# A GRU's x products as seven block products for four steps, with the head's weight transfers and the order of z's sigmoid changed

## The chip, the cores and the metric

The kernel runs on one core of a Trainium2 chip. The metric is the device time of one execution in microseconds (us); the median of three runs is compared. A profiled execution gives the span (first to last instruction of the program) and what every engine did in it: PE is the matrix engine (PEld its weight loads), DVE the vector engine, ACT the scalar engine, POOL the GpSimd engine, SP the engine whose queue issues most transfers.

## The reference

A GRU runs over the 256 time steps of x for 16 sequences with 512 features. Its states go through a router and one expert matrix: each of the 16 experts takes the 256 tokens (of 4096) with the largest router weight, and what they make of them is added to x. The program's own sizes are B = 16, T = 256, D = 512.

```python
def cell(h, x):
    gi = x @ W_ih + b_ih
    gh = h @ W_hh + b_hh
    i_r, i_z, i_n = jnp.split(gi, 3, axis=-1)
    h_r, h_z, h_n = jnp.split(gh, 3, axis=-1)
    r = jax.nn.sigmoid(i_r + h_r)
    z = jax.nn.sigmoid(i_z + h_z)
    n = jnp.tanh(i_n + r * h_n)
    h_new = (1.0 - z) * n + z * h
...
S = jax.nn.softmax(xf @ router_w + router_b, axis=-1)
G, idx = jax.lax.top_k(S.T, k)
out = jnp.einsum('ekh,hd->ekd', xf[idx], expert_w) + expert_b
y = y.at[idx.reshape(-1)].add((G[..., None] * out).reshape(-1, h))
return x + y
```

All of it is float32. The expert's matrix is the same for all experts, so a token's product with it is made once and multiplied by the sum of its gates.

## The kernel before

**Tiling.** Features lie on partitions. The contraction of 512 is four parts k of 128. The matrix engine is used as four column quadrants j of 32: each matmul has 32 stationary columns (or 16 in even steps of the h product), two time steps of 16 sequences, and four of them stand side by side, so that the output's 512 columns fold into 4 x 128. Each float32 matmul is two instructions in the trace. A gate's sums of one pair of steps are a 128 x 128 block of a PSUM bank; the three h banks (r, n, z) hold two such blocks, for even and odd pairs p.

**Head** (L238 to L269, and the block that begins at L443). The weights W_ih (`wih`, four parts k, each in two half transfers by `load_k`) and W_hh (`whh`, three gates, each in two half transfers by `load_gate`) are issued on the queues of SP and ACT, with x's groups 0 and 1 (a group g is eight steps), the state and the biases. PE turns group 0 (`spread_x`), multiplies it by the parts of W_ih as they come (L403), forms the biases, turns group 1 and makes pair 4's product. Pair 5's product is spread over the first four steps of the loop. `make_masks` stands behind the head.

**Loop** (256 steps s; pair p, odd or even; group g, place c in it). The order of PE, ACT, DVE, POOL and SP is the order of the program's text. In a step:

- PE: `h_part` (L426), 96 instructions of 128 columns: gates r and n for the first two k, r and n for the other two, then z for all four. Then half of an x product for the pair six ahead, `x_part` (L403), 16 instructions of 384 columns into `x_bank0` or `x_bank1`. Then units of expert work (`expert`, L370): a unit is one k and a quarter of the columns, 8 instructions of 128. The variable `due` sets how many are made. The next step's h matmuls are queued behind them.
- ACT: r's sigmoid (L505), the copy of the next pair's preset into the r bank (`preset_first`, L386), two halves of tanh (L557), z's sigmoid in one piece (L558), the presets of n and z (`preset_rest`, L389 and L396), `gather` (L293), which copies finished states into `ht`.
- DVE: a one-element copy `seen` (L509) that waits for r, r times h's n in halves (L553), plus x's n (L555), the transposes of n (`turn_n`, L565) and z (`turn_z`, L568), h - n (`less_n`, L571), times z (`by_z`, L576), plus n (`plus_n`, L579), which writes the new state `hs`. Every one of these goes by halves of the features; a step's first h matmuls need half 0, the later ones half 1. Then, every other step, `x_done` (L414), which adds the bias to x's sums and puts them into `ring`, six pairs deep; the transposes of later groups of x (`turn_x`, L228); `expert_done`, which empties expert sums.

Of the 32 groups of tokens, the first 15 (`early_groups`) have their expert product made in the loop; the other 17 (`late_items`) after it by `late_part` (L108): some in quarters of 128 columns beside the search for each expert's smallest chosen weight (`by_bits`), the others, once the gates are known, in 512 columns at a time, from whose sums `store` (L713) writes the output.

Of the kernel before, what the change touches and what calls it, by code (L numbers as in the profile page):

```python
# [17 lines left out]
def kernel(  # L18
# [37 lines left out]
    GH = P // E  # L56
    ident = const.tile([P, P], F32, name="ident")
# [8 lines left out]
    def make_masks():  # L66
# [3 lines left out]
        at = xs[:, RING - 3, 0:3].bitcast(I32)  # L70
# [3 lines left out]
        at_f = xs[:, RING - 2, 0:3]  # L74
        nc.vector.tensor_copy(at_f, at)
        to_i = xs[:, RING - 2, P : 3 * P].bitcast(I32).rearrange("p (o e h) -> p o e h", o=2, h=GH)
        nc.gpsimd.iota(to_i[:, 0, :, :], pattern=[[1, E], [0, GH]], base=0, channel_multiplier=0)
        nc.gpsimd.iota(to_i[:, 1, :, :], pattern=[[0, E], [1, GH]], base=0, channel_multiplier=0)
        to = xs[:, RING - 3, P : 3 * P].rearrange("p (o n) -> p o n", o=2)
# [12 lines left out]
    early_groups = list(range(15))  # L92
# [65 lines left out]
    with (  # L158
# [17 lines left out]
        )  # L176
        rb = wts.tile([P, E], F32, name="rb")

        b_raw = xs[0:2, RING - 8 : RING - 5, :]
        b_n = xs[0:1, RING - 5, :]  # L180
        c0 = xs[0:B, RING - 4, :]
# [15 lines left out]

        def load_rows(dst, src, form):

            rows = src.rearrange(form, c=KC)  # L200
            for h in range(2):
                ks = slice(KC // 2 * h, KC // 2 * (h + 1))
                queues[h].dma_start(out=dst[:, ks, :], in_=rows[:, ks, :])
# [32 lines left out]
        xa2 = xs[:, RING - 9, :].rearrange("p (q d) -> p q d", d=P)  # L236
        with tc.manual_schedule(engines={ET.SP, ET.Activation, ET.Pool}):
            def load_gate(dst, src, form, i, gate):  # L238
                load_rows(dst[:, :, i, :], src[:, gate * D : (gate + 1) * D], form)

            def load_k(k):
                rows = w_ih.rearrange("(p c) n -> p c n", c=KC)
                to = wih.rearrange("p c g d -> p c (g d)")
                for h, queue in enumerate(queues):
                    cols = slice(3 * HD * h, 3 * HD * (h + 1))
                    queue.dma_start(out=to[:, k, cols], in_=rows[:, k, cols])

            nc.sync.dma_start(out=xs[:, 0, :], in_=x[:, 0:TG, :])
            load_k(0)
            nc.scalar.dma_start(out=c0, in_=cond)  # L250
            load_k(1)
            load_k(2)
            nc.scalar.dma_start(out=xs[:, 1, :], in_=x[:, TG : 2 * TG, :])
            load_k(3)
            for gate in (0, 2, 1):
                load_gate(whh, w_hh, "(c p) n -> p c n", gate, gate)
# [7 lines left out]
            for j in range(KC):  # L264
                load_xa(2, xa2, j, (nc.sync, nc.sync))
# [621 lines left out]
```

## Time and profile before

| | us |
|---|---|
| median of 3 runs | 1167.44 (1166.04 to 1168.17) |
| the profiled execution | 1166.15 |
| its span | 1164.4 |
| PE busy, matmuls | 1148.1 (99%) |
| PE busy, weight loads | 925.2 (79%) |
| DVE busy | 769.0 (66%) |
| ACT busy | 387.0 (33%) |
| POOL busy | 42.5 (4%) |
| first h matmul of the loop starts | 26.13 |
| r's sigmoid of the last step starts | 1089.87 |
| the copy of the gates (L707) starts | 1126.35 |

A group line of the page names the source line, engine and operation, output and inputs, shapes and count; then busy time, the mean of one in ns, the engine's idle time ahead of these instructions and what ended most of it. A line of the timeline has the start, the time from the first start to the last end of a merged run of instructions, and the same names; in brackets the idle time ahead of it and its releaser. Matmuls overlap each other: a duration is that of one from start to end, not the distance to the next.

### The profile page before, as it was taken

The numbers are of one execution on the slowest core, as the hardware profiler recorded it, in microseconds if no ns is written. First come the engines' busy times: TensorE is split into PE (matmuls) and PEld (weight loads), VectorE is DVE, ScalarE is ACT, GpSimd is POOL, SyncE is SP. The second block draws the span as 40 slices with busy tenths as digits, with TensorE's granted clock in tenths as the row PEclk, the third lists the DMA queues.
The fourth block names the chain that finished last, engine by engine and source line by source line (L and its number), as shares of the span: only waits on it lengthen the run. The fifth ranks groups of instructions, "written<-read, shape, count | busy, mean of one in ns | idle before, by whom it ended". The sixth has DMA issues, their size and how long they took to land.

```text
span 1164.4 us, 72051 instructions
## 1 busy us (share of the span) xinstructions
PE 1148.1 (99%) x32271; PEld 925.2 (79%) x32271; DVE 769.0 (66%) x4229; ACT 387.0 (33%) x1590; POOL 42.5 (4%) x240
## 2 busy tenths in 40 slices
PE   8999999999999999999999999999999999998898
PEld 4778888888888888888888888888888888888762
DVE  2666667666666666666676666666666666665674
ACT  1233333333333333333333333333333333333420
POOL 1000000000000000000000000000000000000000
PEclk9999999999999999999999999999999999999999
DMA  8100000000000000000000000000000000000126
GB/s 268 38 13 17 21 20 19 16 21 22 20 20 21 19 20 17 21 22 20 20 19 20 19 18 20 22 21 20 20 20 19 20 8 13 4 5 4 48 69 227
DMA packets 43818, 37.02 MB, mean 32 GB/s; under 512 B 6992, under 2 KB 35424, under 8 KB 43504
## 3 DMA queue, kind: packets, MB, share of 16 engines
q1 hardware_dynamic: 41808, 28.89, 8.4%
q8 instruction: 255, 4.18, 1.5%
q10 hardware_dynamic: 1568, 3.44, 0.9%
q14 instruction: 59, 0.48, 0.1%
q0 software_dynamic: 128, 0.02, 0.1%
HBM read 23.94 MB, written 8.39 MB: 28 GB/s over the span
## 4 chain that ended last, share of the span: by engine, by line
PE 95%; DVE 3%; DMA 1%; ACT 1%; issue 0%; SPq 0%; ACTq 0%; DVEq 0%
PE gates L426 57%; PE gates L403 27%; PE pe L108 5%; PE pe L370 5%; DMA wih<-in_L_cond_W_ih_dram 1%; PE gates L305 1%; DVE zT L568 0%; DVE nT L565 0%; DVE t L553 0%; ACT r L505 0%; ACT t L557 0%; DVE hs L579 0%; DVE v L576 0%; PE idle L403 0%; DVE u L571 0%
## 5 line engine op out<-in xcount | busy, mean ns | idle before, releaser
L426 PE MATMUL gates<-whh,hs 128*16 128x128 f32 x24576 | 724.7, 273 | 5.0 <-DVE zT L568 2.5
L426 PEld LDWEIGHTS gates<-whh,hs 128*16 128x16 f32 x24576 | 672.0, 103 | 37.6 <-ACT ht L293 15.8
L403 PE MATMUL gates<-wih,xt 128*32 128x384 f32 x4064 | 379.6, 486 | 1.9 <-DMA wih<-in_L_cond_W_ih_dram 1.6
L505 ACT ACTIVATE r<-gates 128x128 f32<-128x128 f32 x256 | 71.1, 278 | 551.9 <-PE gates L426 551.7
L403 PEld LDWEIGHTS gates<-wih,xt 128*32 128x32 f32 x4064 | 144.4, 110 | 91.4 <-issue 84.3
L509 DVE COPY seen<-r 1x1 f32<-1x1 f32 x256 | 36.3, 142 | 268.0 <-ACT r L505 267.9
L557 ACT ACTIVATE t<-t 128x64 f32<-128x64 f32 x512 | 103.2, 249 | 136.1 <-DVE t L555 136.1
L565 DVE STREAM_TRANSPOSE nT<-t 128x64 f32<-128x64 f32 x512 | 100.4, 234 | 47.8 <-ACT t L557 47.8
L568 DVE STREAM_TRANSPOSE zT<-zs 128x64 f32<-128x64 f32 x512 | 122.7, 240 | 0.6 <-ACT zs L558 0.6
L370 PEld LDWEIGHTS pe<-ewr,ht 128*32 128x32 f32 x1920 | 69.1, 110 | 62.3 <-issue 60.1
L579 DVE TENSOR_TENSOR hs<-v,nT 128x32 f32<-128x32 f32 x512 | 98.3, 192 | 17.4
L576 DVE TENSOR_TENSOR v<-u,zT 128x32 f32<-128x32 f32 x512 | 98.7, 193 | 8.8
L370 PE MATMUL pe<-ewr,ht 128*32 128x128 f32 x1920 | 92.0, 273 | 0.7 <-issue 0.7
L555 DVE TENSOR_TENSOR t<-t,xs 128x64 f32<-128x64 f32 x512 | 90.7, 219 | 0.0
L553 DVE TENSOR_TENSOR t<-r,gates 128x64 f32<-128x64 f32 x512 | 90.3, 218 | 0.0
L571 DVE TENSOR_TENSOR u<-hs,nT 128x32 f32<-128x32 f32 x512 | 78.2, 153 | 0.0
L558 ACT ACTIVATE zs<-gates 128x128 f32<-128x128 f32 x256 | 71.2, 278 | 1.8 <-ACT t L557 0.6
L414 DVE TENSOR_TENSOR xs<-gates,bias 128x384 f32<-128x384 f32 x127 | 69.7, 551 | 0.5 <-PE gates L403 0.5
L108 PE MATMUL pe<-ewr,ht 128*32 128x128 f32 (+2 forms) x1320 | 64.3, 343 | 0.0
L108 PEld LDWEIGHTS pe<-ewr,ht 128*32 128x32 f32 x1320 | 36.9, 110 | 20.5 <-issue 18.5
L293 ACT COPY ht<-hs 128x128 f32<-128x128 f32 (+1 forms) x128 | 52.2, 410 | 0.8 <-DVE hs L579 0.8
L228 DVE STREAM_TRANSPOSE xt<-xa 128x256 f32<-128x256 f32 x58 | 38.7, 668 | 6.5 <-issue 6.5
(106 smaller groups left out, 300.0 us busy)
## 6 DMA issues: line engine op xcount, KB each, us to landing
out_dram<-xs SPq DMA_DIRECT2D x31, 256.0 KB, 3.7
xa<-in_x_dram SPq DMA_DIRECT2D x232, 32.0 KB, 1.9
xs<-in_x_dram SPq DMA_DIRECT2D x100, 64.0 KB, 2.2
xs<-in_x_dram SPq DMA_DIRECT2D x6, 256.0 KB, 3.9
wih<-in_L_cond_W_ih_dram ACTq DMA_DIRECT2D x4, 384.0 KB, 7.9
wih<-in_L_cond_W_ih_dram SPq DMA_DIRECT2D x4, 384.0 KB, 10.7
whh<-in_L_cond_W_hh_dram SPq DMA_DIRECT2D x3, 512.0 KB, 12.8
whh<-in_L_cond_W_hh_dram ACTq DMA_DIRECT2D x3, 512.0 KB, 9.6
```

Of the source, the lines that this page charges most:

```text
L108: nc.tensor.matmul(pe[q, cols], ht[:, g, k, q], ewr[:, k, E:][:, cols], start=False, stop=(k == KC - 1), tile_position=(0, QD * j), skip_g ...
L370: nc.tensor.matmul(pes[g][quadrant(j), at : at + P], ht[:, g, k, quadrant(j)], ewr[:, k, E + P * quarter : E + P * (quarter + 1)], start=F ...
L403: nc.tensor.matmul(bank[quadrant(j), at], lhs, columns(wih[:, k, gates, :].rearrange("p g d -> p (g d)"), j), start=start and k == 0, stop ...
L426: nc.tensor.matmul(dst[quadrant(j, m)], lhs, columns(whh[:, k, gate_, :], j), start=False, stop=(k == KC - 1), tile_position=(0, QD * j), ...
L553: nc.vector.tensor_tensor(t[half], r[:, cols], hn[p % 2][:, cols], ALU.mult)
L555: nc.vector.tensor_tensor(t[half], t[half], ring[:, p % AHEAD, 2, cols], ALU.add)
L557: nc.scalar.activation(t[half], t[half], AF.Tanh)
L565: nc.vector.transpose(nT[half], t[half])
L568: nc.vector.transpose(zT[half], zs[:, halves[half][1]])
L571: nc.vector.tensor_tensor(u[half], hs[:, halves[half][2], slot(s), :], of_step(nT[half], odd), ALU.subtract)
L576: nc.vector.tensor_tensor(v[half], u[half], of_step(zT[half], odd), ALU.mult)
L579: nc.vector.tensor_tensor(hs[:, halves[half][2], slot(s + 1), :], v[half], of_step(nT[half], odd), ALU.add)
```

## The change

- **x products.** For four steps (two pairs, a `quad`), x's 2 x 2 blocks (pairs by halves of the features) times W_ih's 2 x 2 blocks (halves of the features by halves of the columns) are made from seven products of blocks and not eight, in Winograd's form of Strassen's scheme. A product has two k and 192 columns in four quadrants. Sums and differences of weight blocks (`t1`, `t2`, `nt4`, and one in place) are made once in the head on POOL (`mixes`); those of x's blocks for a group of eight steps on DVE (`x_sums`). The partial sums live in five PSUM regions (`a_sum`, `b_sum`, `c_sum`, `d_sum`, `e_sum`), which ACT copies from one to the next and into `ring`; `x_rest` adds the last ones on DVE. `x_done` and the pair-wise `x_part` remain in the head only, for pairs 0 to 3.
- **Expert work.** `early_groups` becomes the first 10 groups. A unit is one k and 384 or 128 columns. `due` grows by 3 in each third step of four, and by 3 or 6 in the last eight steps.
- **z.** Its sigmoid goes by halves, each behind that half's tanh, and the order of DVE's transposes, differences and products is another.
- **Head.** W_ih in four whole transfers, W_hh in three, x's group 1 behind them on SP's queue, the state on POOL's; pair 4's and pair 5's products and the early load of group 2 are gone; `make_masks` stands first.
- **Other moves.** x's transposes, loads, gathers, router products and the emptying of expert sums take place in other steps.

```diff
-    early_groups = list(range(15))
+    early_groups = list(range(N_EARLY))
...
+            nc.gpsimd.dma_start(out=c0, in_=cond)
             nc.sync.dma_start(out=xs[:, 0, :], in_=x[:, 0:TG, :])
-            load_k(0)
-            nc.scalar.dma_start(out=c0, in_=cond)
-            load_k(1)
-            load_k(2)
-            nc.scalar.dma_start(out=xs[:, 1, :], in_=x[:, TG : 2 * TG, :])
-            load_k(3)
-            for gate in (0, 2, 1):
-                load_gate(whh, w_hh, "(c p) n -> p c n", gate, gate)
+            load_k(0, nc.scalar)
+            load_k(1, nc.sync)
+            load_k(2, nc.scalar)
+            load_k(3, nc.sync)
+            load_gate(0, nc.scalar)
+            load_gate(2, nc.sync)
+            load_gate(1, nc.scalar)
+            nc.sync.dma_start(out=xs[:, 1, :], in_=x[:, TG : 2 * TG, :])
...
+        def mixes(part):
+
+            b11, b12 = (wih[:, 0:2].rearrange("p k g d -> p k (g d)")[:, :, cols] for cols in (low, high))
+            b21, b22 = (wih[:, 2:4].rearrange("p k g d -> p k (g d)")[:, :, cols] for cols in (low, high))
+            dst, one, other = ((t1, b12, b11), (t2, b22, t1), (nt4, b21, t2), (b12, b22, b12))[part]
+            nc.gpsimd.tensor_tensor(dst, one, other, ALU.subtract)
+
+        def x_sums(g):
+
+            of = xT[g].rearrange("p (m o) d -> p m o d", o=2)
+            a11, a12, a21, a22 = (of[:, :, o, P // 2 * h : P // 2 * (h + 1)] for o in range(2) for h in range(2))
+            s1, s2, s3, s4 = (sums[:, i] for i in range(4))
+            nc.vector.tensor_tensor(s1, a21, a22, ALU.add)
+            nc.vector.tensor_tensor(s2, s1, a11, ALU.subtract)
+            nc.vector.tensor_tensor(s3, a11, a21, ALU.subtract)
+            nc.vector.tensor_tensor(s4, a12, s2, ALU.subtract)
...
+            dst, lhs, rows = {
+                1: lambda: (a_sum, x_of(quad, 0, 0), at(0, low)),
+                2: lambda: (a_sum, x_of(quad, 0, 1), at(1, low)),
+                3: lambda: (c_sum, s_of(4), at(1, high)),
+                4: lambda: (d_sum, x_of(quad, 1, 1), of(nt4)),
+                5: lambda: (e_sum, s_of(1), of(t1)),
+                6: lambda: (b_sum, s_of(2), of(t2)),
+                7: lambda: (b_sum, s_of(3), at(0, high)),
+            }[i]()
+            for k in range(2):
+                for j in range(KC):
+                    nc.tensor.matmul(
+                        dst[quadrant(j)],
+                        lhs[:, QD * k : QD * (k + 1)],
+                        columns(rows[k], j),
...
+        def x_rest(quad):
+
+            one, two = (ring_of(quad, o, C2) for o in range(2))
+            nc.vector.tensor_tensor(two, b_sum, one, ALU.add)
+            nc.vector.tensor_tensor(one, c_sum, one, ALU.add)
...
-                if x_for:
-                    for k in second if odd else first:
-                        x_part(x_for, k, x_bank)
-                if s < KC:
-                    x_part(AHEAD - 1, s, idles[0], start=False)
...
+                late_four = q4 == 0 and 2 < quad <= NQ
+                if late_four:
+                    x_product(4, quad - 1)
+                if quad < NQ:
+                    for i in ((1,), (2, 5), (6,), (7, 3))[q4]:
+                        x_product(i, quad)
...
                 for half, cols, ks in halves:
                     nc.scalar.activation(t[half], t[half], AF.Tanh)
-                nc.scalar.activation(zs, zz[p % 2], AF.Sigmoid)
+                    nc.scalar.activation(zs[half], zz[p % 2][:, cols], AF.Sigmoid)
...
+                if late_four:
+                    nc.scalar.copy(ring_of(quad - 1, 1), d_sum)
+                if quad < NQ:
+                    if q4 == 0:
+                        nc.scalar.copy(b_sum, a_sum)
+                        nc.scalar.copy(e_sum, spare)
+                    elif q4 == 1:
+                        nc.scalar.copy(ring_of(quad, 0), a_sum)
+                        nc.scalar.copy(a_sum, bias_f[:, 0:C2])
+                    elif q4 == 2:
+                        nc.scalar.copy(c_sum, b_sum)
+                        nc.scalar.copy(ring_of(quad, 0, C2), e_sum)
+                    else:
+                        nc.scalar.copy(d_sum, b_sum)
...
                 for f, half in (
-                    (turn_n, 0), (turn_n, 1), (less_n, 0), (turn_z, 0), (less_n, 1),
-                    (by_z, 0), (plus_n, 0), (turn_z, 1), (by_z, 1), (plus_n, 1),
+                    (turn_n, 0), (turn_z, 0), (less_n, 0), (turn_n, 1), (by_z, 0),
+                    (turn_z, 1), (plus_n, 0), (less_n, 1), (by_z, 1), (plus_n, 1),
                 ):
                     f(half)
```

Here q4 is s % 4, and quad is s // 4 + 2, the four steps whose x product the step works on.

## The prediction

> **What bounds the kernel now.** I read the page first (chain and groups), then when the gate sigmoid r starts in each of the 256 steps, then single steps in the timeline, then the end of the program.
>
> ```profile
> PE 95%; DVE 3%; DMA 1%; ACT 1%; issue 0%; SPq 0%; ACTq 0%; DVEq 0%
> ...
> L426 PE MATMUL gates<-whh,hs 128*16 128x128 f32 x24576 | 724.7, 273 | 5.0 <-DVE zT L568 2.5
> ...
> L403 PE MATMUL gates<-wih,xt 128*32 128x384 f32 x4064 | 379.6, 486 | 1.9 <-DMA wih<-in_L_cond_W_ih_dram 1.6
> ```
>
> The chain lies on PE for 95%, and PE hardly ever waits (5.0 us before L426 in the whole run). Read alone, this says that less PE work is less time. The last steps of the loop, which have no x product and no expert work left, say something else (timeline, PE and ACT lines):
>
> ```profile
> 1079.79 2.83 PE L426 MATMUL gates<-whh,hs 128*32 128x128 f32 x96 [1.22 <-DVE zT L568]
> ...
> 1081.36 0.28 ACT L505 ACTIVATE r<-gates 128x128 f32<-128x128 f32 x1 [1.58 <-PE gates L426]
> ...
> 1083.88 2.81 PE L426 MATMUL gates<-whh,hs 128*16 128x128 f32 x96 [1.27 <-DVE zT L568]
> ...
> 1085.44 0.28 ACT L505 ACTIVATE r<-gates 128x128 f32<-128x128 f32 x1 [2.43 <-PE gates L426]
> ```
>
> PE stands idle 1.22 and 1.27 us in each of these, and still r comes 4.08 us after r (1081.36 to 1085.44); the even step before it (1067.16 to 1071.20) took 4.04. That is the recurrence's own time: h products, sigmoid, tanh, transposes, new state. A step in mid-run with the x product takes the same 4.08 (605.29 to 609.37); with one expert unit more it takes 4.13. All 255 distances sum to 1062.1 us, 4.165 on average. So PE and recurrence are nearly level, the recurrence at 4.06 (mean of 4.04 and 4.08) close below PE. Taking PE work out can win at most (4.165 - 4.06) x 255 = 27 us here; a longer recurrence costs 255 times its growth. Its second half is this:
>
> ```profile
> 605.29 0.28 ACT L505 ACTIVATE r<-gates 128x128 f32<-128x128 f32 x1 [1.84 <-PE gates L426]
> ...
> 606.25 0.40 ACT L557 ACTIVATE t<-t 128x64 f32<-128x64 f32 x2 [0.68 <-DVE t L555]
> 606.34 1.50 PE L403 MATMUL gates<-wih,xt 128*32 128x384 f32 x16
> 606.54 0.39 DVE L565 STREAM_TRANSPOSE nT<-t 128x64 f32<-128x64 f32 x2 [0.18 <-ACT t L557]
> ...
> 606.66 0.28 ACT L558 ACTIVATE zs<-gates 128x128 f32<-128x128 f32 x1
> ...
> 606.85 0.15 DVE L571 TENSOR_TENSOR u<-hs,nT 128x32 f32<-128x32 f32 x1
> 606.97 0.24 DVE L568 STREAM_TRANSPOSE zT<-zs 128x64 f32<-128x64 f32 x1
> ...
> 607.14 0.15 DVE L571 TENSOR_TENSOR u<-hs,nT 128x32 f32<-128x32 f32 x1
> 607.25 0.19 DVE L576 TENSOR_TENSOR v<-u,zT 128x32 f32<-128x32 f32 x1
> 607.48 0.19 DVE L579 TENSOR_TENSOR hs<-v,nT 128x32 f32<-128x32 f32 x1
> 607.59 0.24 DVE L568 STREAM_TRANSPOSE zT<-zs 128x64 f32<-128x64 f32 x1
> ```
>
> z's sigmoid starts at 606.66, 1.37 us after r (1.31 in the even step, 601.16 to 602.47): z is the last of the 96 h matmuls, and the x matmuls follow at 606.34 with the last h matmuls still under way for 0.27 (their duration in L426), so until 606.61. It waits for PE, not for tanh. Then zT, the other u, v, and at 607.48 the first half of the new state, which starts the next step's matmuls at 607.81.
>
> At the end of the program PE is the bound (PEld lines of the timeline):
>
> ```profile
> 1127.14 0.13 PEld L108 LDWEIGHTS pe<-ewr,ht 128*32 128x32 f32 x4 [0.30 <-issue]
> 1127.57 0.13 PEld L108 LDWEIGHTS pe<-ewr,ht 128*32 128x32 f32 x4 [0.30 <-issue]
> 1128.00 0.13 PEld L108 LDWEIGHTS pe<-ewr,ht 128*32 128x32 f32 x4 [0.30 <-issue]
> ```
>
> Four 512-column expert matmuls every 0.43 us, nearly without a gap from 1126.25 to 1158.5, while the stores wait for their sums.
>
> **x products: off PE, but hardly on the path.** Matmuls run in fours. A four of 128 columns takes 0.109 us (96 from 607.81 until x follows at 610.43: 2.62 / 24), one of 384 takes 0.323 (16 in 610.43 to 611.72). Three times the columns, three times the time, so 192 columns lie between at 0.161. A product is two k and four quadrants, each float32 matmul two instructions: 16, so 0.65. Four steps had 64 x 384 columns (5.16 us) and get seven products (4.52): 0.64 less. The steps hold two, two, one and two products (the fourth runs a step late, beside the next four's first), and three expert units (24 x 128 columns, 0.65) go to the one with one. So PE is busy 2.62 + 1.30 = 3.92 in every step: under any recurrence of 4 us or more. The Trainium skill speaks against cutting: "TensorEngine Tiling (Array Packing)", section Instruction Overhead, has some 60 cycles on top of each matmul. An estimate by it, at the 2.4 GHz of the skill's page "Trainium Kernel Development and Optimization" (section NeuronCore Architecture): two products would add 32 x 25 ns / 4 = 0.2 us, which makes a step's PE 4.12 and leaves it beneath the recurrence worked out below. The two rows show no such term, and the sum goes by them.
>
> **The copies of the sums.** Eight ACT copies of 192 columns per four steps, between 0.27 (128 columns, L386) and 0.38 (256, L130): 0.33. The fullest step has three, the first behind a product's end. They are queued after both halves of z; last to end is product 1, 2.62 + 1.30 + 0.3 after the step's first matmul, then two copies, 0.7 at most: 0.8 us ahead of the next r (1.57 after the next first matmul). Cover, price 0. Were it gone, r would be late, then tanh, then the state. On DVE, x_done (0.55 every other step) goes; two sums of 192 columns per four steps and four of 128 per eight come, under 1.2 us in one step, in the 1.6 us between the new state and the next r. Pool's mixing of the weights (4 instructions of 1536 elements) has no row: at its iota of 128 columns (0.38), 4.6 us each, 9 if two inputs double it. It starts near 8 us, and its results are wanted at 31 to 43 us: 0, at worst 2. The Trainium skill's "GPSIMD Engine Reference" (section Elementwise — side-by-side cycle accounting) has 4497 ns for such an addition of 2048 elements, an estimate of 3.4 us for 1536, which would make it 0 as well. The fourth waits until the head's x matmuls have read the weights.
>
> **z's halves and the new DVE order: on the path.** ACT now runs tanh 0, z 0, tanh 1, z 1. z 0 still needs the last h matmul: it starts no earlier than z does now, and tanh 1 stands behind it. Gain: a 64-column activation takes 0.24 (second tanh) and not 0.28, so zT 0 starts 0.04 to 0.05 earlier. Loss: DVE then has u 0, nT 1, v 0, zT 1 ahead of the state's sum. Distances from start to start, from the rows above and the even step: zT to u 0.17, u to the next transpose 0.08 (602.72 to 602.80), transpose nT 1 to what follows 0.15 (the pair from 606.54 lasts 0.39, its second some 0.23, so it starts at 606.70; u at 606.85), v to a transpose 0.11 (as hs to zT, 607.48 to 607.59), zT to hs 0.16 (as zT to u at 602.80 to 602.96). Sum 0.67, against 0.51 today (606.97 to 607.48). Net +0.12 a step: 4.06 becomes 4.18. Bounds: 0 if the order costs nothing, +0.16 if z's halves gain nothing. I take 4.175.
>
> **Loop.** 255 x 4.175 = 1064.6. Extra: three steps with five units and one product (PE 4.36, 0.19 each), seven where less_max (1.14 us at 1093.16) and turn_x (0.67) share a step's 1.6 us (0.2 each), 0.4 in the last two: 2.4. Together 1067.0 against 1062.1: **+4.9**.
>
> **Tail.** Ten early groups and not fifteen: five more go to L108 after the gate is known. Each is 16 matmuls, 32 instructions, 8 fours at 0.43 = 3.44: **+17.2** (lower bound 0 if the tail had room; rows give none, as the output's DMA ends with PE).
>
> **Head.** h starts at 26.13. Removed: pair 4's x product, 32 matmuls, 2.7 us on PE. The weights come as whole transfers; the 2.25 us wait for the second (12.24) may shrink by 1.5. Added ahead of the first preset on DVE: one subtraction, 0.3. What is late next is x_done and the presets on ACT behind spread_x, which keep the start near 23.5: **-2.6**. But x's second group is now the last on SP's queue, behind three weight transfers (k 1, k 3, gate 2), with 6.8 MB in all ahead of or beside it; at the 370 to 400 GB/s of the filled slices it lands near 20, just when its transposes are due. Bounds -3 and +1.
>
> **Sum:** 1164.4 - 2.6 + 4.9 + 17.2 = 1183.9 of span. The profiled run took 1166.15, 1.75 beside its span: 1185.65. It is 1.3 under the median of 1167.44, so against the median some 1186: **1186**, 1.6% slower.
>
> **Rivals.** (1) Faster: z's halves and the order cost nothing, the step stays at 4.06: 255 x 4.06 + 2.4 = 1037.7, total 1157. The mechanism is slack on DVE between nT and zT that takes up the new order; it decides below 4.10 a step, where the loop wins back the 14.6 of tail and head and its own 2.4 (17.0 / 255 = 0.067 under 4.165). For it: DVE is busy 66%. Against it: its instructions stand in order, and three of those counted come behind zT 0. (2) Slower still: the copies or the sums hold up r or the state by 0.1 a step: 25 us, 1211. For it: ACT waits for products in its queue; against it: 0.8 us of cover. (3) 192 columns cost more than their share: at 0.22 a four, steps with two products have 2.62 + 1.76 = 4.38, three of four steps, +0.2 x 191 = 38 us, 1224. Against: the two rows on either side.
>
> **How the numbers follow.** Forecast (1175 to 1197: step 4.14 to 4.21, head -3 to +1) 0.62; rival 1 0.13; between it and the forecast 0.10; rivals 2 and 3 0.15. The range 1166 to 1204 leaves out most of rival 1 and the far half of 2 and 3. A median of this kernel tells some 0.2% from no change (2.3 us): faster 0.13, same 0.05, slower 0.82.
>
> **What would show it.** r to r at 4.15 to 4.20 with PE idle before the h matmuls in most steps, released by DVE hs or zT; 16 matmuls of 192 columns in 0.65; zs 0 starting 1.31 to 1.37 after r; from zT 0 to the first hs 0.67; the gate's copy to the last expert matmul 17 us longer; first r near 25. Wrong if the step is under 4.10, if PE is as gapless as before, or if r waits for an ACT copy.

## The result and the profile after

The changed kernel took 1179.95 us (median of 4 runs, 1178.66 to 1181.74), the kernel before beside it 1166.74: a ratio of 1.0116, 95% interval 1.0094 to 1.0138. It is slower by 1.2%; forecast were 1186 and 1.6%, with a range of 1166 to 1204. The profiled execution has a span of 1177.7 us, 13.3 more than before. The two traces, stretch by stretch (r is the sigmoid of a step, the distances are from start to start):

| stretch | before | after | difference | forecast |
|---|---|---|---|---|
| start to r of step 0 | 27.76 | 29.97 | +2.2 | -2.6 |
| r of step 0 to r of step 255 | 1062.11 | 1056.02 | -6.1 | +4.9 |
| of it, 255 undisturbed steps at | 4.069 | 4.085 | +4.1 | +29 (4.175 for 4.06) |
| of it, first distance and all else above that | 24.5 | 14.3 | -10.2 | -24 |
| r of step 255 to the gate's copy | 36.48 | 36.50 | 0 | 0 |
| gate's copy to the end of PE | 32.57 | 49.74 | +17.2 | +17.2 |

An undisturbed step is read as the level that the 15% shortest distances lie under, even and odd steps apart (before 4.051 and 4.087, after 4.063 and 4.107).

The page of the changed kernel: the chain by engine, and the groups of h's matmuls, their weight loads, z's sigmoid and the block products:

```profile
PE 94%; DVE 3%; DMA 2%; ACT 1%; issue 0%; ACTq 0%; DVEq 0%
...
L489 PEld LDWEIGHTS gates<-whh,hs 128*16 128x16 f32 x24576 | 666.9, 103 | 94.9 <-ACT gates L648 27.7
L489 PE MATMUL gates<-whh,hs 128*16 128x128 f32 x24576 | 734.4, 274 | 9.2 <-DVE u L673 5.1
...
L635 ACT ACTIVATE zs<-gates 128x64 f32<-128x64 f32 x512 | 112.9, 220 | 32.4 <-PE gates L489 20.3
L462 PE MATMUL gates<-wih,xt 128*32 128x192 f32 x1984 | 111.5, 327 | 0.5 <-issue 0.4
```

The chain still lies on PE, and PE's idle time ahead of h's matmuls is 9.2 us in all. The weight loads, which come first, wait 94.9 us: a page that calls PE the bound hides that a third of a microsecond is open in nearly every step. That is easier to see in one step (timeline, all engines):

```profile
604.37 0.28 ACT L579 ACTIVATE r<-gates 128x128 f32<-128x128 f32 x1 [1.13 <-PE gates L489]
...
605.31 0.58 PEld L462 LDWEIGHTS gates<-xs 128*32 128x32 f32 x16
...
605.67 0.22 ACT L635 ACTIVATE zs<-gates 128x64 f32<-128x64 f32 x1
605.79 0.25 ACT L634 ACTIVATE t<-t 128x64 f32<-128x64 f32 x1
605.91 0.51 PEld L308 LDWEIGHTS gates<-ht,ewr 128*16 128x16 f32 x16
605.93 0.25 DVE L670 STREAM_TRANSPOSE zT<-zs 128x64 f32<-128x64 f32 x1
...
606.33 0.15 DVE L678 TENSOR_TENSOR v<-u,zT 128x32 f32<-128x32 f32 x1
...
606.56 0.15 DVE L681 TENSOR_TENSOR hs<-v,nT 128x32 f32<-128x32 f32 x1
...
606.82 1.28 PEld L489 LDWEIGHTS gates<-whh,hs 128*32 128x32 f32 x48 [0.40 <-ACT gates L648]
```

The sixteen matmuls of a product load from 605.31, the next work from 605.91: 0.60 to 0.65 for a product, as forecast. The next step's first load waits 0.40 and follows the state (606.56). The releaser named there, an ACT copy that ended at 606.73, is not one that h's first matmuls need: the load follows the end of the state (606.71) by 0.11, as it does where no such copy is near. From the start of zT to the first half of the state it is 0.63, where 0.67 was forecast and 0.51 was measured before.

At the end of the program PE's loads stand as they did before, four 512-column matmuls every 0.43 us, for five groups more:

```profile
1123.28 0.13 PEld L110 LDWEIGHTS pe<-ewr,ht 128*32 128x32 f32 x4 [0.30 <-issue]
1123.71 0.13 PEld L110 LDWEIGHTS pe<-ewr,ht 128*32 128x32 f32 x4 [0.30 <-issue]
1124.14 0.13 PEld L110 LDWEIGHTS pe<-ewr,ht 128*32 128x32 f32 x4 [0.30 <-issue]
```

The head went against the forecast. Busy times by stretch (PE, PEld, DVE, ACT, POOL, then the granted clock, the DMA share and GB/s):

```profile
20.00:23.00 3.00, 1.56 (x20) 0.39 (x12) 0.00 (x0) 0.00 (x0) 3.00 (x2) 1.00 1.04 333
23.00:25.00 2.00, 0.75 (x4) 0.58 (x5) 0.83 (x5) 0.00 (x0) 2.00 (x1) 1.00 1.09 364
25.00:26.00 1.00, 0.59 (x2) 0.10 (x1) 1.00 (x2) 0.00 (x0) 1.00 (x2) 0.98 0.49 164
26.00:28.00 2.00, 0.91 (x20) 0.74 (x24) 2.00 (x6) 0.81 (x3) 0.24 (x1) 0.50 0.16 47
28.00:30.00 2.00, 2.00 (x44) 1.61 (x40) 0.96 (x5) 0.03 (x1) 0.00 (x0) 0.50 0.03 9
```

PE has little to do from 21.5 to 27.1: it waits 1.83 for x's group 1, then for DVE, then for presets. The granted clock falls to 0.50 from 26.0 to 32.8. The first h matmul starts at 27.09 (before 26.13), r follows it by 2.88 instead of 1.6, and the first distance between r's is 5.25 (before 4.50).

### The profile page after: what moved, and what is told of

Its sections match the earlier page's. It is cut to its first block, busy times and chain, and to the rows that moved or that the text cites. A ratio compares the mean times of both kernels' runs of the same rounds, so it can differ in the third digit from the quotient of the medians.

```text
span 1177.7 us, 76649 instructions
## 1 busy us (share of the span) xinstructions
PE 1154.3 (98%) x34125; PEld 994.6 (84%) x34125; DVE 754.6 (64%) x4344; ACT 548.6 (47%) x2343; POOL 51.8 (4%) x218
## 3 DMA queue, kind: packets, MB, share of 16 engines
q8 instruction: 270, 4.42, 1.5%
## 4 chain that ended last, share of the span: by engine, by line
PE 94%; DVE 3%; DMA 2%; ACT 1%; issue 0%; ACTq 0%; DVEq 0%
PE gates L489 61%; PE gates L462 23%; PE pe L110 7%; PE pe L371 3%; DMA xs<-in_x_dram 2%; DVE zT L670 1%; ACT zs L635 0%; DMA wih<-in_L_cond_W_ih_dram 0%; DVE u L673 0%; PE gates L308 0%; DVE nT L667 0%; DVE v L678 0%; DVE hs L681 0%; PE bank L774 0%; DVE xs L546 0%
## 5 line engine op out<-in xcount | busy, mean ns | idle before, releaser
L489 PEld LDWEIGHTS gates<-whh,hs 128*16 128x16 f32 x24576 | 666.9, 103 | 94.9 <-ACT gates L648 27.7
L579 ACT ACTIVATE r<-gates 128x128 f32<-128x128 f32 x256 | 71.1, 278 | 266.7 <-PE gates L489 266.7
L634 ACT ACTIVATE t<-t 128x64 f32<-128x64 f32 x512 | 129.2, 252 | 137.8 <-DVE t L632 137.8
L670 DVE STREAM_TRANSPOSE zT<-zs 128x64 f32<-128x64 f32 x512 | 122.8, 240 | 27.1 <-ACT zs L635 1.3
L635 ACT ACTIVATE zs<-gates 128x64 f32<-128x64 f32 x512 | 112.9, 220 | 32.4 <-PE gates L489 20.3
L462 PE MATMUL gates<-wih,xt 128*32 128x192 f32 x1984 | 111.5, 327 | 0.5 <-issue 0.4
L462 PE MATMUL gates<-xs 128*32 128x192 f32 x1984 | 110.9, 326 | 0.2 <-issue 0.2
L462 PE MATMUL gates<-wih,xs 128*32 128x192 f32 x1984 | 96.2, 326 | 0.0
L462 PEld LDWEIGHTS gates<-wih,xt 128*32 128x32 f32 x1984 | 75.3, 110 | 7.3 <-issue 2.3
L462 PEld LDWEIGHTS gates<-xs 128*32 128x32 f32 x1984 | 76.1, 110 | 5.1 <-issue 1.5
L462 PEld LDWEIGHTS gates<-wih,xs 128*32 128x32 f32 x1984 | 75.7, 110 | 3.7 <-issue 0.5
L110 PEld LDWEIGHTS pe<-ewr,ht 128*32 128x32 f32 x1480 | 42.1, 110 | 32.5 <-issue 30.7
L462 PE MATMUL gates<-xs,xt 128*32 128x192 f32 x992 | 54.1, 326 | 0.0
```

The lines of the kernel that those rows point to most:

```text
L110: nc.tensor.matmul(pe[q, cols], ht[:, g, k, q], ewr[:, k, E:][:, cols], start=False, stop=(k == KC - 1), tile_position=(0, QD * j), skip_g ...
L462: nc.tensor.matmul(dst[quadrant(j)], lhs[:, QD * k : QD * (k + 1)], columns(rows[k], j), start=False, stop=(k == 1), tile_position=(0, QD ...
L489: nc.tensor.matmul(dst[quadrant(j, m)], lhs, columns(whh[:, k, gate_, :], j), start=False, stop=(k == KC - 1), tile_position=(0, QD * j), ...
L634: nc.scalar.activation(t[half], t[half], AF.Tanh)
L635: nc.scalar.activation(zs[half], zz[p % 2][:, cols], AF.Sigmoid)
L670: nc.vector.transpose(zT[half], zs[half])
```

## The experiments

Medians are given with the ratio to the kernel before, which ran beside each (1166.33 us for the first four, 1165.83 for the next four, 1166.00 for the three after them, 1166.17 for the last). "Drifted" is a step in whose h pass the last four matmuls, one for each column quadrant, start over more than 0.08 us; in an undisturbed step it is 0.03 to 0.05. Before has 15 such steps, the changed kernel 51, which cost it 9.7 us.

### The kernel before with ten early groups

```diff
-    early_groups = list(range(15))
+    early_groups = list(range(10))
```

> The kernel before with 10 early groups and not 15, nothing else changed. Theory (the tail's growth is the five moved groups alone): from the copy of the gates to the end 38.0 us becomes 55.2; the first r stays at 27.76; the loop gives back the last 80 units, some 85 steps by 0.055 and 3 us at its end, so -5 to -8. Together +9 to +13, 1176 to 1180 us. Rival (the changed kernel's tail is long for another reason, buffers or the later loads of x): this tail grows by less than 8 us and the time stays under 1170.

1177.17 us, ratio 1.0091 (1.0073 to 1.0110). From the gate's copy to the end of PE 49.74, the loop 1055.32. The whole tail is the five groups, and they alone make most of the result: +10.8 of some 13. The loop gives back 6.8 of the 17.2; the first r comes 0.8 sooner (26.97), which was not expected and stays unexplained. And 1055.3 is what the changed loop takes as well (1056.0): as they stand, the seven products win nothing over the plain ones with the same expert work.

### The kernel before with z by halves

```diff
-                nc.scalar.activation(zs, zz[p % 2], AF.Sigmoid)
+                    nc.scalar.activation(zs[half], zz[p % 2][:, cols], AF.Sigmoid)
...
-                    (turn_n, 0), (turn_n, 1), (less_n, 0), (turn_z, 0), (less_n, 1),
-                    (by_z, 0), (plus_n, 0), (turn_z, 1), (by_z, 1), (plus_n, 1),
+                    (turn_n, 0), (turn_z, 0), (less_n, 0), (turn_n, 1), (by_z, 0),
+                    (turn_z, 1), (plus_n, 0), (less_n, 1), (by_z, 1), (plus_n, 1),
```

> The kernel before with only the change of z: its sigmoid by halves behind each tanh, and the new order of DVE. Theory (from the changed kernel's trace, where the bare step is 4.06 and 4.11, mean 4.085): the recurrence grows by 0.025 a step, and most of it is hidden under PE's 4.09 to 4.13: 0 to +4 us. Rival (the prediction's count of DVE distances, +0.115 a step): step 4.15 to 4.20, +6 to +10 us.

1167.16 us, ratio 1.0006 (0.9993 to 1.0018). The undisturbed step is 4.087 for 4.069, +0.02 and not +0.115. The loop does not move (1062.12 for 1062.11): there PE's work still covers it.

### The changed kernel with z whole and DVE's old order

The same diff backwards, on the changed kernel.

> The changed kernel with z's sigmoid whole and the DVE order of before. Theory: bare steps at 4.04 and 4.08, 255 x 0.025 = 6 us less, some 1174. Rival (the prediction's +0.115): 29 us less, some 1151. Second rival (z's halves help once PE is off the path): slower than the changed kernel.

1177.28 us, ratio 1.0090 (1.0070 to 1.0110). The step goes from 4.085 to 4.063, the loop from 1056.0 to 1053.4, with 60 drifted steps: 0.022 a step is 5.6 us, of which 2.9 went into a greater loss by drift (12.6 for 9.7), so the whole time falls by 2.7 and not by the expected 6. So z's halves and their order cost 0.02 a step in either kernel.

### The changed kernel with u ahead of zT

```diff
-                    (turn_n, 0), (turn_z, 0), (less_n, 0), (turn_n, 1), (by_z, 0),
-                    (turn_z, 1), (plus_n, 0), (less_n, 1), (by_z, 1), (plus_n, 1),
+                    (turn_n, 0), (less_n, 0), (turn_z, 0), (by_z, 0), (turn_n, 1),
+                    (plus_n, 0), (turn_z, 1), (less_n, 1), (by_z, 1), (plus_n, 1),
```

> The changed kernel with another order on DVE: u 0 ahead of zT 0, v 0 right behind it, then nT 1, the state's sum, zT 1, u 1, v 1, the second sum. Theory (DVE takes its instructions in order, so what stands between zT 0 and the first half of the state is on the path): from zT 0 to hs 0.63 becomes 0.50 to 0.54, the step 3.99 to 4.02, 17 to 24 us less, some 1160. Rival (PE with 3.92 a step and what its quadrants lose is the next bound): 5 us less at most.

1172.53 us, ratio 1.0044 (1.0030 to 1.0058). The step is 4.040, the loop 1047.9, and the time falls by 7.4 us, where 17 to 24 were expected: the step did not reach 3.99 to 4.02, and 61 drifted steps cost 13.3 us, 3.6 more than in the changed kernel. DVE and ACT in one step (timeline):

```profile
601.59 0.19 DVE L673 TENSOR_TENSOR u<-hs,nT 128x32 f32<-128x32 f32 x1
...
601.70 0.24 DVE L670 STREAM_TRANSPOSE zT<-zs 128x64 f32<-128x64 f32 x1
...
601.97 0.19 DVE L678 TENSOR_TENSOR v<-u,zT 128x32 f32<-128x32 f32 x1
602.08 0.24 DVE L667 STREAM_TRANSPOSE nT<-t 128x64 f32<-128x64 f32 x1
...
602.24 0.15 DVE L681 TENSOR_TENSOR hs<-v,nT 128x32 f32<-128x32 f32 x1
```

From zT to the state it is 0.54 and not 0.63. It shows why the forecast's sum was too large, too: v waits here for the transpose just ahead of it and lasts 0.19, while in the changed order, with a transpose of n between, it lasts 0.15. So of the 0.08 us that an instruction in between costs, 0.04 comes back in the next one. This is a version of z's halves that does shorten the recurrence.

### Expert weights held back

```diff
-            nc.sync.dma_start(out=ewr[:, :, E:], in_=expert_w.rearrange("(c p) n -> p c n", c=KC))
-            nc.sync.dma_start(out=ewr[:, :, 0:E], in_=router_w.rearrange("(c p) n -> p c n", c=KC))
-            nc.sync.dma_start(out=eb, in_=expert_b.rearrange("(o d) -> o d", o=1).to_broadcast([P, D]))
...
+                    if s == 0:
+                        nc.sync.dma_start(out=ewr[:, :, E:], in_=expert_w.rearrange("(c p) n -> p c n", c=KC))
+                        nc.sync.dma_start(out=ewr[:, :, 0:E], in_=router_w.rearrange("(c p) n -> p c n", c=KC))
+                        nc.sync.dma_start(out=eb, in_=expert_b.rearrange("(o d) -> o d", o=1).to_broadcast([P, D]))
```

> The changed kernel with the expert's and the router's weights and the bias (1.3 MB) issued in the first step of the loop, not in the head. Theory (these transfers, no longer held back on SP's queue, take bytes from the recurrent weights and x's second group): x's group lands about 3 us sooner, PE's idle time ahead of its transposes falls from 1.83 to under 0.5, the granted clock stays at 1.00 and not 0.50 from 26 to 32 us, the first r comes at 26 to 28 and not 29.97, the first step takes 4.1 and not 5.26: 3 to 5 us less. Rival (the group's last place on SP's queue alone): unchanged.

1181.90 us, ratio 1.0136 (1.0119 to 1.0153). Nothing came: x's group 1 is turned at 23.63 (23.38 before the edit), h starts at 27.01, the clock is 0.50 from 26.0 to 32.8. The theory that the expert weights hold up x's group falls.

### And x's group 1 asked for ahead of the last gates

```diff
             load_k(3, nc.sync)
+            nc.sync.dma_start(out=xs[:, 1, :], in_=x[:, TG : 2 * TG, :])
...
             load_gate(1, nc.scalar)
-            nc.sync.dma_start(out=xs[:, 1, :], in_=x[:, TG : 2 * TG, :])
```

> The same, and x's second group ahead of gate 2 on SP's queue. Theory (what is late after that is the recurrent weights): PE never waits for x's group, the clock stays at 1.00, the first r at 25 to 26.5, 4 to 6 us under the changed kernel. Rival (the weights of gate 2 land at the same time as before and the first h matmuls wait for them instead): no better than the kernel that only holds the expert's weights back.

1181.56 us, ratio 1.0129 (1.0112 to 1.0145). Now x's group is turned at 21.16 without a wait, and h still starts at 26.76. What took the wait's place stands on DVE (timeline, DVE lines, and then POOL's):

```profile
22.75 3.12 DVE L543 TENSOR_TENSOR xs<-bias 128x192 f32<-128x192 f32 x1
25.80 1.47 DVE L411 TENSOR_TENSOR xs<-gates,bias 128x384 f32<-128x384 f32 x3
```

```profile
15.28 7.00 POOL L427 TENSOR_TENSOR xs<-wih,xs 128x1536 f32<-128x1536 f32 x2
22.25 3.41 POOL L427 TENSOR_TENSOR wih<-wih 128x1536 f32<-128x1536 f32 x1
```

The new subtraction of 192 columns takes 3.12 us and ends when POOL's last mix ends (25.66). Instructions of the same size with one input in PSUM take 0.36 in the loop. Both inputs of this one lie in SBUF. In the changed kernel itself it takes 1.23, because x's group is late and hides the rest.

### TensorE's idle stretches filled

```diff
+            keep_clock(6, (idles[1],))
             spread_x(1, idles[0])
...
             keep_clock(2)
+            keep_clock(4, (idles[1],))
```

> The changed kernel with ten more filling matmuls on PE in the head (six ahead of the transposes of x's second group, four ahead of the first h matmuls), transfers as in the changed kernel. Theory (the clock falls because PE stands idle between 21.5 and 27): the clock stays at 1.00, r follows the first h matmul by 1.57 and not 2.88, the first step takes 4.1: 2 to 2.6 us less. Rival (the clock falls for another reason, or the first h pass is slow because weights are late): no change, clock 0.50 or a first step over 5 us as before.

1191.35 us, ratio 1.0199 (1.0171 to 1.0227). The head does what the theory says: the clock stays at 1.00, r of step 0 comes at 28.58 and the first distance is 4.00, 2.6 us in sum. But the loop, in which nothing was changed, takes 1069.59 with 87 drifted steps, which cost 23.6 us. Ten matmuls in the head made a loop of 256 later steps slower; that was the clue to what the drift is.

### Fifteen early groups in the changed kernel

```diff
-    N_EARLY = 10
+    N_EARLY = 15
...
-                for cols in (slice(0, 3 * P), slice(3 * P, D))
+                for cols in quarters
...
-                        due += 3 if q4 == 2 else 0
+                        due = min(4, due + (1, 1, 3, 0)[q4])
```

> The changed kernel with 15 early groups: units of 128 columns, one in the first two steps of four, three in the third. Theory (PE has 0.16 of slack in a bare step): the tail loses 17.2 us; a unit of 0.22 in a step with two products stretches it by 0.05, 108 steps: +6 us; together 1167 to 1171. Rival (PE has no slack, as its quadrants drift apart when it is filled): each unit costs 0.22, nothing gained, 1178 or more.

1180.33 us, ratio 1.0118 (1.0100 to 1.0136). The tail is back at 32.57, but the loop takes 1074.8, 18.8 more. That is close to the 80 units' own time on PE (80 x 0.218 = 17.4), as the rival has it, but the trace puts most of it elsewhere. 13 of the 18.8 lie in steps that end drifted or have a gap over 0.13 us in their h pass (65 steps, 22.9 us above the undisturbed step; in the changed kernel 52 steps, 9.8 us). In ten of them PE stops within the pass, with 0.45 to 1.28 us from the start of one matmul to the next, 7.5 us in sum (timeline, PE lines of one):

```profile
702.06 2.78 PE L489 MATMUL gates<-whh,hs 128*16 128x128 f32 x91
705.65 0.29 PE L489 MATMUL gates<-whh,hs 128*16 128x128 f32 x3 [0.81 <-issue]
```

In the other steps, one with two products and a unit is 0.08 to 0.10 above the undisturbed step (median and mean of 71): less than half of a unit's 0.22, and more than the theory's 0.05. So the open third of a microsecond does take much of a unit, and what spoils this kernel is mostly drift and these stops; the next section shows where they stand.

### The same filling in small matmuls

What is drift? PE's code is itself brought by DMA. The DMA table of the changed kernel has a queue for it:

```profile
q8 instruction: 270, 4.42, 1.5%
```

270 packets and 4.42 MB are 16 KB a packet, and PE has 68,567 recorded instructions: 254 a packet, so a block holds 256. The Trainium skill has the same size ("Runtime: NRT & Kernel Launch", section Instruction fetch mechanics). It also says there that the fetch is hidden, since the engine issues more slowly than the blocks come. I numbered PE's recorded instructions from the first one and took the gaps inside the h passes of steps 1 to 254 (over 0.111 us from the start of one matmul to the next; 0.109 is what one quadrant that is a matmul late leaves). All 32 in the changed kernel stand at numbers 193 to 205 modulo 256; before all 6 at 193 to 208, with u ahead of zT 35 of 36. In all the runs of this text together it is 301 of 303, at 193 to 208 (the expectation below counts by a lower limit and has 33 of 37 at 184 to 207, and 257 instructions a step). A step of the changed loop has some 255 instructions, so the same place of the step meets this place of the block for dozens of steps in a row. A step before has some 241 and wanders over the whole block.

25 of these gaps are stops of over 0.3 us, the ten of the kernel with fifteen groups among them. All stand at number 193 or 194, and 24 of them end 1.2 to 1.5 us after a code packet has landed, which points to code that came late. The short ones end 1.3 to 2.6 us after one, with no such tie.

```diff
+            fill(14, 208)
             spread_x(1, idles[0])
...
             keep_clock(2)
+            fill(11, 176)
...
+        def fill(fours, n):
+            for _ in range(fours):
+                for j in range(KC):
+                    nc.tensor.matmul(
+                        idles[1][quadrant(j), 0:n],
+                        zero[:, 0:QD],
+                        zero[:, 0:E].unsqueeze(1).to_broadcast([P, n // E, E]),
+                        start=True,
+                        stop=True,
+                        tile_position=(0, QD * j),
+                        skip_group_check=True,
+                    )
```

> The changed kernel with the same idle stretches of the head filled as in the run that filled them with ten wide bf16 matmuls (1191.35 us), for about the same time, but with 100 small ones (32 weight columns each, in fours: 14 fours of 208 columns, 11 fours of 176). Theory: TensorE's code comes in blocks of 16 KB (the DMA table: 270 packets, 4.42 MB, for some 68,600 recorded TensorE instructions, so 256 of them a block), and at one fixed place of each block its stream has a short hole. The irregular gaps inside h's passes stand at instruction number 184 to 207 modulo 256 in every kernel so far (33 of 37 in this change's own trace between 184 and 207), and the changed loop has about 257 instructions a step, so that the same place of the step is hit for many steps in a row. The wide filling moved every step on by 20 instructions, into more hits (87 steps drifted, 23.6 us); 100 matmuls with their 100 weight loads move it on by 200, which is back by 56: h's passes then begin at about 72 to 169 modulo 256, where the traces show some 0.01 us a step lost. Then under 15 drifted steps, loop 1045 to 1051 us instead of 1069.6, first h at 26.9, step 0's r at 28.6, whole time 1167 to 1173. Rival: the full clock or the filling itself, or the loads of x, make the quadrants drift: some 85 drifted steps, loop 1066 to 1073, whole time 1187 to 1194.

1169.81 us, ratio 1.0031 (1.0019 to 1.0043); loop 1046.38, 11 drifted steps. In this kernel and the next, the small matmuls open new sums in part of a PSUM bank that early groups use afterwards, so that part of the expert sums is not the reference's; no instruction of the loop or of the tail is missing. The head's filling did not do all of its work (the clock is 0.50 from 26 to 28, r of step 0 at 29.60), and the loop is 23.2 us shorter than with the wide filling all the same. Two steps of the changed kernel, one after the other, and two of this one (timeline, PE lines):

```profile
271.98 2.84 PE L489 MATMUL gates<-whh,hs 128*32 128x128 f32 x94
274.60 0.36 PE L462 MATMUL gates<-wih,xs 128*32 128x192 f32 x2
274.65 0.28 PE L489 MATMUL gates<-whh,hs 128*32 128x128 f32 x2
...
276.21 2.93 PE L489 MATMUL gates<-whh,hs 128*16 128x128 f32 x94
```

```profile
241.91 2.81 PE L489 MATMUL gates<-whh,hs 128*16 128x128 f32 x96
244.53 0.85 PE L462 MATMUL gates<-xs,xt 128*32 128x192 f32 x16
...
245.96 0.32 PE L489 MATMUL gates<-whh,hs 128*32 128x128 f32 x4
```

In the first, two x matmuls start ahead of the last two of the h pass: one quadrant is behind the others, and r waits for it; the next pass starts 4.23 later. In the second all 96 come before any x, and the next pass starts 4.05 later. By the place in the block at which a step's h pass starts (steps; of them drifted; us lost above the undisturbed step):

```
                      place 64 to 175      place 176 to 239
changed               121,  6,  2.3        121, 45, 11.3
wide filling  (+20)    74,  9,  1.3        158, 76, 24.9
small filling (-56)   225,  3,  1.8         13,  5,  1.5
```

The loss goes by the place. The rival, that the filling causes the drift, is out: more matmuls of filling, and 76 fewer drifted steps. That the full clock does is out with the last two runs below: the clock is 1.00 in the head of both, with 57 drifted steps in one and 15 in the other.

### Small filling and u ahead of zT

The last diff and DVE's order from above.

> The same filling, and VectorE's order with u of half 0 ahead of zT (bare step 4.040 measured, 1172.53 us as a whole, loop 1047.94 with 61 drifted steps that cost 13.3). Theory of the code blocks: loop 1034 to 1039, under 15 drifted steps, distance of the first two r's 4.0 instead of 5.3, whole time 1155 to 1162, faster than before by 0.4 to 1 per cent. Rival (the drift does not go by instruction numbers): loop 1055 to 1063 with some 85 drifted steps, whole time 1178 to 1186.

1160.66 us, ratio 0.9953 (0.9941 to 0.9966); loop 1035.83, 11 drifted steps, first distance 3.99. All as expected, and the first version ahead of the kernel before.

### The subtraction with one input from PSUM

```diff
-            nc.vector.tensor_tensor(spare, bias_f[:, C2 : 2 * C2], bias_f[:, 0:C2], ALU.subtract)
+            nc.vector.tensor_tensor(spare, l_bank[:, C2 : 2 * C2], bias_f[:, 0:C2], ALU.subtract)
```

on the kernel with x's group 1 asked for early.

> The run with the expert weights held and x's group 1 asked for early (1181.56 us), and in it the one subtraction that stood beside GpSimd's last mix (VectorE, 128x192, both inputs in SBUF, 3.12 us instead of some 0.4) takes its first input from PSUM, where the same bias still lies. Theory: it was the two SBUF inputs beside GpSimd's tensor operation that held it. Then it takes 0.36 to 0.5, the sums and presets behind it come 2.7 us earlier, first h at 23.7 to 24.5, and with TensorE's gap shorter the granted clock stays 1.00: step 0's r at 25.3 to 26.2, distance of the first two r's 4.1, whole time 1176 to 1179. Rival: VectorE waits for the mix or for a shared buffer in any case: the subtraction stays near 3 us, first h at 26.8, whole time 1181 to 1183.

1178.36 us, ratio 1.0111 (1.0096 to 1.0126), against 1.0129 without this edit. DVE's lines, and POOL's last mix:

```profile
22.84 0.35 DVE L543 TENSOR_TENSOR xs<-gates,bias 128x192 f32<-128x192 f32 x1
23.10 1.94 DVE L411 TENSOR_TENSOR xs<-gates,bias 128x384 f32<-128x384 f32 x4
24.96 0.97 DVE L434 TENSOR_TENSOR xs<-xt 128x128 f32<-128x128 f32 x1
25.96 0.29 DVE L435 TENSOR_TENSOR xs<-xs,xt 128x128 f32<-128x128 f32 x1
```

```profile
22.34 3.44 POOL L427 TENSOR_TENSOR wih<-wih 128x1536 f32<-128x1536 f32 x1
```

The subtraction takes 0.35 beside the same mix. The first instruction after it with both inputs in SBUF (L434) is held in its place, 0.97 until the mix is over, where the next of its kind takes 0.29. h starts at 24.07, the clock stays at 1.00, r of step 0 comes at 25.72. The first distance is 4.36, not 4.1, and the second 5.95, as PE stops within that h pass (1.76 us from one matmul to the next), at number 194 of the block. The loop keeps 57 drifted steps, as it should without a filling. The Trainium skill has the conflict ("GPSIMD Engine Reference", section Key points: GpSimd shares its SBUF interfaces with VectorE and contends with VectorE instructions that have two SBUF inputs). The rows agree, and show for how long here: until the end of a 3.4 us operation.

### All of it together

The head of the run with the PSUM operand, u ahead of zT, and the small matmuls in another place, now opening no sums (start=False):

```diff
-            keep_clock(8)
+            keep_clock(2)
+            fill(26, 96)
```

> All that held so far in one kernel: the head of the run with the PSUM operand (step 0's r at 25.72 there), VectorE's order with u of half 0 ahead of zT (step 4.040), and the small matmuls, now in place of six of the eight wide ones that TensorE does before x's first group lands: 26 fours of 96 columns and 196 instructions more in sum, 60 back modulo 256. Theory: place in the 16 KB block alone counts, wherever the instructions are put; step 0's r at 25.7 to 26.2, distance of the first two r's 4.0 to 4.4, loop 1034 to 1039 with under 15 drifted steps, whole time 1155 to 1159, ratio to before 0.990 to 0.994. Rival: without a filling just ahead of h the drift is back: some 60 drifted steps, loop 1046 to 1050, whole time 1167 to 1171.

1163.01 us, ratio 0.9968 (0.9956 to 0.9979): faster than before, but short of the expected 1155 to 1159. Head and place are about as expected: r of step 0 at 26.23, 15 drifted steps, and from step 20 on the steps lose 4.4 us above the undisturbed one, where they lose 4.8 with small filling and u ahead of zT (1160.66). The loop takes 1043.69, not 1034 to 1039. The miss is the first ten steps, where six distances of 4.6 to 5.6 follow one another (with a later one of 4.71, 7.3 us) (timeline, PE lines):

```profile
38.83 2.78 PE L486 MATMUL gates<-whh,hs 128*32 128x128 f32 x90 [0.50 <-DVE zT L682]
42.67 0.38 PE L486 MATMUL gates<-whh,hs 128*32 128x128 f32 x4 [1.06 <-issue]
```

PE stops for 1.06 us within a pass of 96 with nothing to wait for that the profile shows. There are five such stops in these steps, all at number 193 or 194 of the block. The code packets come at 34.2, 40.4, 45.3, 50.3 and 55.4, one for each, and PE goes on 1.3 to 1.5 us after each has landed. From 30 to 34 the held expert weights fill the DMA engines (share 0.81 and 1.10). That they put the code late is the likely reading of why it comes so often here; it was not tried apart, the kernel with fifteen groups has such stops in mid-run, and in the run of 1160.66, with the weights issued in the head, the same steps took 4.03 to 4.05.

## Why the prediction was right, and where it was not

**The tail** was right: +17.17 for +17.2, and the first experiment shows that it is the five groups and nothing else.

**The products' price on PE** was right. A four of 192 columns takes 0.162 (0.65 for a product), an addition per matmul is not seen, and rival 3 is out. The copies of the sums cost nothing: ACT, which makes them, stands idle ahead of each of the 256 r's, for 0.28 us at least, and all this time (266.7 us) is put down to PE's h matmuls; rival 2 is out.

**z's halves and DVE's order** had the right sign and the wrong size. The step that failed is "Net +0.12 a step: 4.06 becomes 4.18"; measured are +0.016 between the traces and +0.02 in both experiments. Between the run with z whole and the changed kernel, in undisturbed steps, zT 0 starts 0.06 sooner after r (forecast 0.04 to 0.05: a half of z's sigmoid lasts 0.22 and not "0.24"); from there to the start of the state's first half it takes 0.12 longer (forecast 0.16); and that sum itself is 0.04 shorter, which the forecast put at nothing. v and the state's sum last 0.15 where they no longer start directly behind the result that they need; the distances added up came from rows where they do, at 0.19. By the forecast's own sign ("Wrong if the step is under 4.10") this part was wrong.

**The loop's extra** was mis-sized the other way: "Together 1067.0 against 1062.1", with 2.4 beside the steps. The extra is 14.3 (1056.02 less 255 x 4.085), most of it drift from PE's code blocks, which no step of the forecast had. Both errors together made the loop 11 us shorter than forecast. So the step was near rival 1's 4.06, and rival 1 still did not come: what the step won, drift, head and tail took. Its own condition (faster below 4.10) rested on the same 2.4.

**The head** was wrong in sign: "x_done and the presets on ACT behind spread_x, which keep the start near 23.5: -2.6". Two things were to be read and were not put together. x's second group was named as last on its queue and put at 20; it landed near 23. And POOL's mixes were cleared by their end alone ("its results are wanted at 31 to 43 us: 0"), not asked what they do to an instruction beside them on DVE. The third, the halved clock, followed from the gaps that these two made. It was +2.2 to the first r, and +0.8 in the first distance.

**The sum** of 1186 was 6 us off: -11 in the loop and +5 in the head. The sign of the result stood on the tail, which the forecast had right to a tenth; the closeness of the whole is partly luck.

The change does bring something that its own time does not show. With plain products and ten groups the loop takes 1055.3; with seven products away from the bad place of the code block 1046.4, and with u ahead of zT 1035.8. What is left open is what holds PE in the short gaps at 193 to 208, and whether the place can be moved by other means than the count of instructions.

## What to carry to other kernels

When a loop that was not touched gets slower after an edit ahead of it, count the engine's instructions modulo one code block (256 here): a step of nearly a whole block meets the same place for dozens of steps, and instructions ahead of the loop move it (here 200 more moved it away, and 20 more made it worse). Work put on an idle engine has to be checked against what runs beside it, not only against when its results are wanted. Work put off from a loop to the stage behind it has two prices: here the loop won 6.8 us and the tail lost 17.2.

## What the hardware showed that was not expected

- PE's code comes in packets of 16 KB, and its stream has a weak place: of 303 gaps over 0.111 us inside h's passes in all the runs, 301 stand at 193 to 208 modulo 256 of the recorded instructions. Drifted steps cost 9.7 us in the changed kernel, 23.6 with 20 more instructions ahead of the loop, 2.4 with 200 more. The fetch is not always hidden here, other than the skill's page says.
- DVE's subtraction of 192 columns with both inputs in SBUF took 3.12 us beside a POOL operation, and 0.35 with one input from PSUM.
- The granted clock fell to 0.50 at 26.0, for 6.8 us, in a stretch in which PE was busy 1.9 of 6 us (21 to 27), though none of its gaps was longer than 1.83. The Trainium skill ("TensorE: Matmul & The Clock Gate", section What's actually happening) has the half clock after an idle window of some 3.4 us; this trace shows none so long.
- A short DVE instruction (128x32) lasts 0.15 us where what it needs was done in good time, and 0.19 where it starts directly behind the end of what it needs (one, the second u of the changed order, lasts 0.18 without that).
